# The scan's decays in PSUM, its C rows in SBUF, and one bank for the first stage's matmuls: a two-layer Mamba, attention and expert kernel

## The chip, the cores and the metric

The kernel runs on one core of a Trainium2 chip. Its time is device microseconds from launch to end. Five engines take part: PE (TensorE, matmuls), DVE (VectorE), ACT (ScalarE), POOL (GpSimd) and SP (SyncE, which issues most DMAs). Each works through its own queue in order, and they wait for one another through semaphores. SBUF is the working memory; PSUM is the small memory of eight banks that matmuls write into, and which DVE and ACT can read and write, too. One bank holds a tile of 128 partitions x 512 float32 values.

## What is computed

Eight batch rows of 512 tokens with 256 channels pass two layers. Layer 0 is a gate-and-average conditioning, a Mamba block, a per-row linear map and a mixture of 8 experts (top 2). Layer 1 is a LoRA-modified feed-forward, attention with 8 heads, an adapter with layer norm, and a mixture of 32 experts (top 4). The change touches the scan of the Mamba block:

```python
delta = jax.nn.softplus(jnp.einsum('blr,dr->bld', dt, W_dt) + b_dt)
A = -jnp.exp(A_raw)

def step(h, inp):
    x_t, dlt, B_t, C_t = inp
    dA = jnp.exp(dlt[:, None, :] * A[None])
    h = dA * h + dlt[:, None, :] * B_t[:, :, None] * x_t[:, None, :]
    y_t = jnp.einsum('bn,bnd->bd', C_t, h) + D * x_t
    return (h, y_t)
...
_, ys = jax.lax.scan(step, h0, xs)
y = ys.transpose(1, 0, 2) * jax.nn.silu(z)
return jnp.einsum('bld,md->blm', y, W_out)
```

There are 512 inner channels (index d) and 16 states (index n), so 8192 recurrences over 512 time steps for each batch row.

## The kernel before

**Threads.** Two generators are woven together. `thread_x` does the conditioning and the Mamba block of one row after another and writes the result to `xa[b]`. `thread_y` takes the rows in groups [0], [1, 2], [3, 4, 5], [6, 7] through the rest of layer 0 and the attention. While `thread_y` works on one group, the main loop advances `thread_x` through the next group in proportion to the costs that both yield. After the last group of `thread_x`, `top4`'s routes take its place beside `thread_y`; the expert tiles and the gathers of the last mixture end the program. Within `thread_x`, `scan(b)` of one row is woven with `head(b + 1)` of the next: two steps of the head at each yield of the scan, and what is left of the head before item 58 of the scan.

The text order is not yet the order on an engine. The program's framework puts the instructions into the engines' queues when the program is built, by their dependencies, their place in the text and the buffers that are free; in the trace 174 of the 512 scans stand directly behind another scan on DVE, though the text alternates scan and product.

**The scan.** A row's work has 64 items (j, g, k): j is a quarter of the channels (128), g a quarter of the states (4), k a quarter of the 128 channels (32). An item is a tile of 128 partitions (4 states x 32 channels) x 512 time steps.

- `begin(i)` (L619) issues, two items ahead, the decay `dA = exp(delta * A)` on ACT (L623) into one of four SBUF buffers, and `h = (delta * x) * B` on POOL (L625) into one of eight `h` buffers. Both read `packed`, a tile that a DMA has spread over the four state groups (L595, `get_pack`). The B row spread over the partitions, `B4`, comes from `get_B4` (L598): a matmul of the selection matrix `states(g)` with the row's B and C values (`bc3`, bfloat16) into a `gx` bank, then a copy on ACT (L603) into SBUF. It is made once for each g of a row and kept over the four j.
- `run(i)` (L645) issues the recurrence on DVE (L651, `tensor_tensor_scan`, in place over `h`) and the product with the C row (L652). The C row is spread by a matmul for every j and g into the one PSUM bank `c4` (L649, L650), so 16 times for each row, and read there by four products.
- `add(i)` (L654) sums over the states after each four items: four matmuls with `fold` into a quarter each of the bank `yp` (L660). After the last g, DVE adds D x (L664) and POOL multiplies with silu(z) (L665).

**The head.** `head_a` and `head_b` make the next row's inputs of the scan. Each matmul result goes through `gx()` (L373), a PSUM tile of a ring of two banks, and is read by ACT or DVE: 19 such tiles in `head_a` (eight of them for the averages, read by DVE at L475), 13 in `head_b`. `scan` takes two more at its end for `W_out`, and `get_B4` four for each row.

**PSUM.** The pool `psx` of `thread_x` has four banks: `gx` twice, `c4` and `yp`. The pool of `thread_y` has the other four: `g` twice and `acc` twice. The routes of `top4` use `psx` after `thread_x`: `gx` as a ring of two (L938), `yp` and `c4` for the shared expert's sums (L985).

Of the kernel before, what the change touches and what calls it, by code (L numbers as in the profile page):

```python
# [10 lines left out]
F32 = mybir.dt.float32  # L11
I32 = mybir.dt.int32
AF = mybir.ActivationFunctionType
ALU = mybir.AluOpType
# [3 lines left out]
P = 128  # L18
# [33 lines left out]
def adaln_attn_ffn_kernel(ctx: ExitStack, tc: tile.TileContext, d: dict, out: bass.AP):  # L52
# [314 lines left out]
    def thread_x(wp, wk, ps):  # L367
# [3 lines left out]
            return t  # L371

        def gx():  # L373
            return ps.tile([P, T], F32, tag="gx", name="gx", bufs=2)

        rows = {}

# [206 lines left out]
        def states(g):  # L584
            return quads[:, g].rearrange("k n c -> k (n c)")

        packs = [dram.tile([4, P, 2, T], F32, name=f"pack{i}", tag=f"pack{i}") for i in range(2)]
        xzs = [dram.tile([P, 4, 2, T], F32, name=f"xzs{i}", tag=f"xzs{i}") for i in range(2)]
        got, B4s = {}, {}

        def get_pack(b, j, k):

# [2 lines left out]
            nc.sync.dma_start(t, src[None].to_broadcast([4, 32, 2, T]))  # L595
            got[b, j, k] = t

        def get_B4(b, g):  # L598

            pt = gx()  # L600
            mm(pt, [(states(g), rows[b])])
            t = wk.tile([P, T], F32, tag="B4", name="B4", bufs=4)
            nc.scalar.copy(t, pt)  # L603
            B4s[b, g] = t


        fold = wp.tile([P, 32], F32, tag="fold", name="fold")
# [3 lines left out]

        def scan(b):

            bc3 = rows[b]
            items = [(j, g, k) for j in range(4) for g in range(4) for k in range(4)]
            yps, Cs, hs, dAs, xz = {}, {}, {}, {}, {}
            y8 = wk.tile([P, 4, T], F32, tag="y8", name="y8")

            def begin(i):  # L619
                j, g, k = items[i]  # L620
                t = got[b, j, k]
                dA = wk.tile([P, T], F32, tag="dA", name="dA", bufs=4)
                nc.scalar.activation(dA, t[:, 0, :], AF.Exp, scale=A[:, 4 * j + k, g : g + 1])  # L623
                h = wk.tile([P, T], F32, tag="h", name="h", bufs=8)
                nc.gpsimd.tensor_tensor(h, t[:, 1, :], B4s[b, g], ALU.mult)  # L625
                hs[i], dAs[i] = h, dA
                if (g, k) == (1, 0):
                    xz[j] = wk.tile([P, 2, T], F32, tag="xz", name="xz")
                    nc.sync.dma_start(xz[j], xzs[b % 2][:, j])
                if j == 0 and g < 3 and k == 1:  # L630
                    get_B4(b, g + 1)

                if j < 3 and (g, k) == (2, 3):
                    get_pack(b, j + 1, 0)
                if j < 3 and g == 3 and k < 3:
                    get_pack(b, j + 1, k + 1)
                if j == 3 and b + 1 < NB and g == 3:
                    if k == 0:
                        get_pack(b + 1, 0, 0)
                    if k < 3:  # L640
                        get_pack(b + 1, 0, k + 1)
                    if k == 3:
                        get_B4(b + 1, 0)

            def run(i):  # L645
                j, g, k = items[i]
                h = hs[i]
                if k == 0:
                    Cs[0] = ps.tile([P, T], F32, tag="c4", name="c4")  # L649
                    mm(Cs[0], [(states(4 + g), bc3)])  # L650
                nc.vector.tensor_tensor_scan(h, dAs.pop(i), h, 0.0, ALU.mult, ALU.add)  # L651
                nc.vector.tensor_tensor(h, h, Cs[0], ALU.mult)  # L652

            def add(i):  # L654

                j, g, k = items[i]
                if g == 0:
                    yps[j] = ps.tile([P, T], F32, tag="yp", name="yp")
                for k in range(4):
                    nc.tensor.matmul(  # L660
                        yps[j][32 * k : 32 * k + 32, :], fold, hs.pop(i + k), start=(g == 0), stop=(g == 3))
                if g == 3:
                    y = wk.tile([P, T], F32, tag="tr", name="y", bufs=2)
                    nc.vector.scalar_tensor_tensor(y, xz[j][:, 0, :], col("D", j), yps.pop(j), ALU.mult, ALU.add)  # L664
                    nc.gpsimd.tensor_tensor(y8[:, j, :], xz.pop(j)[:, 1, :], y, ALU.mult)  # L665

            begin(0)
            begin(1)
            for i in range(64):
                if i == 58:  # L670
                    yield from after[0]
                if i < 62:
                    begin(i + 2)
                run(i)
                if i % 4 == 0 and i > 0:
                    add(i - 4)
                if i % 2:
                    yield 5
            add(60)
            x = wk.tile([P, KC, T], F32, tag="gm", name="xr")  # L680
            nc.sync.dma_start(x, d["x"][b])
            for e in range(KC):
                pt = gx()
                mm(pt, [(W_out[:, j, ts(e, P)], y8[:, j, :]) for j in range(4)])
                nc.vector.tensor_tensor(x[:, e, :], x[:, e, :], pt, ALU.add)
            nc.sync.dma_start(xa[b], x)
            yield 3
# [6 lines left out]
        yield from head_b(0)  # L694
        for k in range(4):
            get_pack(0, 0, k)
        get_B4(0, 0)

        def head(b):
            yield from head_a(b)  # L700
# [228 lines left out]
    def top4(wp, wk, ps):  # L929
# [5 lines left out]
            nc.sync.dma_start(sh[n], d[n])  # L935

        def ps_tile():
            return ps.tile([P, T], F32, tag="gx", name="g4", bufs=2)  # L938

        xs = []  # L940
        counts = Counts(wp, E4)
        def route(b):
            x = wp.tile([P, KC, T], F32, tag=f"x{b}", name=f"x{b}")
            nc.sync.dma_start(x, xb[b])
            xs.append(x)
            s = dynamic(b, 1)
            dw = wk.tile([P, KC, P], F32, tag="dw", name="dw")
            nc.sync.dma_start(dw, d["dw"][bass.ds(s, 1)].rearrange("s p k o -> p (s k) o"))
            uw = wk.tile([P, C], F32, tag="uw", name="uw")
            nc.sync.dma_start(uw, d["uw"][bass.ds(s, 1)].rearrange("s p o -> p (s o)"))  # L950
            av = wk.tile([P, 7], F32, tag="av", name="av")
            nc.sync.dma_start(av, d["av"][bass.ds(s, 1)].rearrange("s p o -> p (s o)"))
            pt = ps_tile()
            mm(pt, [(dw[:, k, :], x[:, k, :]) for k in range(KC)])
            z = wk.tile([P, T], F32, tag="z", name="z")
            nc.scalar.activation(z, pt, AF.Relu, bias=av[:, 0:1])
            yield 1
            y = wk.tile([P, KC, T], F32, tag="y", name="y4")
            for e in range(KC):
                pt = ps_tile()  # L960
                mm(pt, [(uw[:, ts(e, P)], z)])
                nc.vector.scalar_tensor_tensor(y[:, e, :], pt, av[:, 1 + e : 2 + e], x[:, e, :], ALU.add, ALU.add)
            yield 1
            c, rstd = yield from layernorm(wk, ps_tile, y, bufs=2)
            yield 1
            for k in range(KC):
                nc.vector.scalar_tensor_tensor(c[:, k, :], c[:, k, :], av[:, 3 + k : 4 + k], rstd, ALU.mult, ALU.mult)
                nc.vector.tensor_scalar(c[:, k, :], c[:, k, :], av[:, 5 + k : 6 + k], None, ALU.add)

            yield 1  # L970
            pt = ps_tile()
            lp = pt[:, 0 : 4 * E4].rearrange("p (a e) -> p a e", a=4)
            for a in range(4):
                mm(lp[:, a, :], [(c[:, k, ts(a, P)], gW[:, k, :]) for k in range(KC)])
            pr = softmax(wk, lp, E4, 1.0)
            top = wk.tile([P, 4, 8], F32, tag="top", name="top")
            ti = wk.tile([P, 4, 8], U32, tag="ti", name="ti")
            for a in range(4):
                nc.vector.max(top[:, a, :], pr[:, a, :])
                nc.vector.max_index(ti[:, a, :], top[:, a, :], pr[:, a, :])  # L980
            nc.vector.tensor_copy(wts4[:, b], top[:, :, 0:K4])
            yield from dispatch(b, c, ti, dest4, counts, wk, ps_tile, ps_tile, E4, K4, CAP4, tab4, "tab4")

            yield 1
            yp = [ps.tile([P, T], F32, tag=t, name="y4p") for t in ("yp", "c4")]  # L985
            for f in range(KC):
                pa = ps_tile()
                mm(pa, [(sh["Ws1"][:, k, ts(f, P)], c[:, k, :]) for k in range(KC)])
                pb = ps_tile()
                mm(pb, [(sh["Ws3"][:, k, ts(f, P)], c[:, k, :]) for k in range(KC)])  # L990
                a = wk.tile([P, T], F32, tag="a", name="a4", bufs=2)
                nc.scalar.activation(a, pa, AF.Silu)
                nc.vector.tensor_tensor(a, a, pb, ALU.mult)
                for k in range(KC):
                    nc.tensor.matmul(yp[k], sh["Ws2"][:, f, ts(k, P)], a, start=(f == 0), stop=(f == KC - 1))
                yield 1
            for k in range(KC):
                nc.vector.tensor_tensor(x[:, k, :], x[:, k, :], yp[k], ALU.add)
# [202 lines left out]
```

## Time and profile before

| what | value |
|---|---|
| median of 3 runs | 4290.34 us (4277.67 to 4293.29) |
| the profiled execution | 4282.53 us, of which its span is 4280.8 us |
| busy PE, DVE, ACT, POOL | 3470.1, 2667.8, 1683.1, 1570.6 us |
| mean granted TensorE clock | 0.886 |
| scans (L651) | 512, first at 145.5 us, last at 2924.8 us |
| decays (L623) | 512, 720 ns each, and 86 table loads of 1283 ns |
| B copies (L603) | 32, 578 ns each |
| fold matmuls (L660) | 1024 |

The span is the time from the first to the last instruction that the profiler saw. An engine's busy time is the union of its instructions' times. In a cost group, the two numbers behind the first bar are the busy time of all and the mean time of one in ns; behind the second bar is the time that the engine stood idle before them, and which instruction's end released it. "PE" is matmuls, "PEld" the weight loads ahead of them.

The rows follow each other so: head 0 alone to 145.5 us; scan 0 with head 1 to 392.8; from there scans 1 to 7 with later heads and `thread_y`, the scans starting at 392.7, 716.2, 1047.0, 1396.4, 1746.9, 2087.6 and 2611.7 us; the routes and the last group of `thread_y`; and from about 3850 us the last expert tiles and gathers.

### The profile page before, as it was taken

The page shows a single profiled execution, that of the slowest core. Times are in us where ns is not written, and L with a number is a line of the kernel's source. Part 1 is how long each engine was busy: PE and PEld are TensorE (multiplying, and loading weights), DVE is VectorE, ACT ScalarE, POOL GpSimd, SP SyncE. Part 2 cuts the span into 40 slices and gives each one's busy share as a digit, 9 for nine tenths or more (in the row PEclk, how much of TensorE's full clock was granted, in tenths as well). Part 3 has the DMA queues.
Part 4 walks back from the last instruction along what each step waited for, and adds up shares of the span by engine and source line. Part 5 has one row for each costly group of instructions (what it writes and reads, how often), then busy time and mean ns, then how long its engine had stood idle before and what let it go on. Part 6 is the DMA issues. An engine that isn't in the chain of part 4 may idle for free. (4 is left out here: it accounts for less than half of the span.)

```text
span 4280.8 us, 36836 instructions
## 1 busy us (share of the span) xinstructions
PE 3470.1 (81%) x10964; PEld 1699.2 (40%) x10964; DVE 2667.8 (62%) x4276; ACT 1683.1 (39%) x2753; POOL 1570.6 (37%) x1222
## 2 busy tenths in 40 slices
PE   4557686888687888888858898889988999977994
PEld 2111352332254233333327443333456444436773
DVE  5698957987866686796791547565432354443336
ACT  2535463454355345346433443332223243222222
POOL 0456535435536334433552323231043211124552
PEclk7668798898798898999879998999999999989996
DMA  3325445234446423333346312213043212117776
GB/s 104 120 91 194 180 153 172 99 116 165 161 162 210 140 100 117 128 117 106 138 169 226 125 62 70 74 35 104 15 160 137 90 44 70 36 44 243 249 239 221
DMA packets 159372, 554.78 MB, mean 130 GB/s; under 512 B 27730, under 2 KB 34289, under 8 KB 146756
## 3 DMA queue, kind: packets, MB, share of 16 engines
q1 hardware_dynamic: 135076, 501.35, 34.8%
q0 software_dynamic: 24096, 51.08, 3.2%
q8 instruction: 87, 1.43, 0.1%
q14 instruction: 113, 0.93, 0.1%
HBM read 453.00 MB, written 234.82 MB: 161 GB/s over the span
## 5 line engine op out<-in xcount | busy, mean ns | idle before, releaser
L625 POOL TENSOR_TENSOR h<-packed,B 128x512 f32<-128x512 f32 x512 | 790.7, 1566 | 1045.0 <-PE yp L660 669.6
L651 DVE TENSOR_TENSOR_SCAN h<-dA,h 128x512 f32<-128x512 f32 x512 | 799.0, 1585 | 142.8 <-POOL h L625 77.3
L623 ACT ACTIVATE dA<-packed,Aexp 128x512 f32<-128x512 f32 x512 | 360.5, 720 | 676.5 <-DVE h L651 468.1
L160 POOL DMA_INDIRECT tok<-ys,to_i x310 | 312.5, 1008 | 494.4 <-DVE ys L808 228.1
L660 PE MATMUL yp<-h,fold 128*32 128x512 f32 x1024 | 355.2, 710 | 166.2 <-DVE h L652 151.8
L922 PE MATMUL acc<-aT,V 128*128 128x512 f32 x1024 | 454.4, 598 | 8.2 <-ACT aT L906 4.9
L160 POOL DMA_INDIRECT tab<-row,si x192 | 199.6, 1040 | 463.0 <-DVE si L250 170.0
L652 DVE TENSOR_TENSOR h<-h,c 128x512 f32<-128x512 f32 x512 | 329.8, 672 | 24.2 <-PE c L78 23.3
L922 PEld LDWEIGHTS acc<-aT,V 128*128 128x128 f32 x1024 | 193.2, 191 | 248.9 <-issue 236.0
L78 PE MATMUL acc<-wv,c 128*128 128x512 f32 x512 | 276.2, 655 | 2.7 <-DVE aT L906 2.0
L78 PE MATMUL g<-qk 64*128 64x512 f32 x512 | 228.2, 673 | 59.1 <-ACT qk L871 32.0
L892 DVE TENSOR_REDUCE nm<-g 128x1 f32<-128x512 f32 x256 | 170.2, 681 | 122.4 <-PE g L78 121.3
L895 ACT ACTIVATE ex<-g,nm 128x512 f32<-128x512 f32 x256 | 175.0, 686 | 163.8 <-DVE nm L892 162.6
L78 PE MATMUL g<-xT,fw 128*128 128x256 f32 x960 | 234.4, 396 | 0.4 <-ACT h L801 0.4
L78 PE MATMUL acc<-fw,h 128*128 128x256 f32 x960 | 221.6, 383 | 4.1 <-DVE ys L808 2.4
L78 PEld LDWEIGHTS g<-xT,fw 128*128 128x128 f32 x960 | 187.8, 200 | 38.7 <-issue 8.0
L905 PEld LDWEIGHTS acc<-ident,ex 128*128 128x128 f32 x1024 | 126.5, 149 | 188.1 <-issue 69.7
L78 PEld LDWEIGHTS acc<-fw,h 128*128 128x128 f32 x960 | 182.6, 192 | 42.4 <-issue 12.2
L905 PE MATMUL acc<-ident,ex 128*128 128x128 f32 x1024 | 163.8, 291 | 41.2 <-ACT V L879 26.8
L660 PEld LDWEIGHTS yp<-h,fold 128*32 128x32 f32 x1024 | 45.2, 116 | 374.4 <-DVE h L652 217.6
L479 DVE TENSOR_TENSOR_SCAN tr<-alpha,gm 128x512 f32<-128x512 f32 x128 | 182.4, 1442 | 7.4 <-POOL y L665 7.1
L78 PE MATMUL g<-xT,mw 128*128 128x256 f32 x760 | 183.9, 386 | 0.0
(280 smaller groups left out, 5437.8 us busy)
## 6 DMA issues: line engine op xcount, KB each, us to landing
fw<-in_fW SPq DMA_DIRECT2D x60, 1154.0 KB
tab<-zeros SPq DMA_DIRECT2D x32, 2112.0 KB
packed<-pack SPq DMA_DIRECT2D x128, 512.0 KB
mw<-in_mW SPq DMA_DIRECT2D x95, 384.0 KB
tab<-zeros SPq DMA_DIRECT2D x16, 2080.0 KB
xt<-tab SPq DMA_DIRECT2D x95, 264.0 KB
xz<-xzs SPq DMA_DIRECT2D x32, 512.0 KB
pack<-dd SPq DMA_DIRECT2D x32, 512.0 KB
```

Of the source, the lines that this page charges most:

```text
L78: nc.tensor.matmul(o, lhsT, rhs, start=(i == 0), stop=(i == len(pairs) - 1))
L160: i = nc.gpsimd.indirect_dma_start(out=table_, out_offset=bass.IndirectOffsetOnAxis(ap=idx, axis=0), in_=src, in_offset=None, bounds_check ...
L479: nc.vector.tensor_tensor_scan(tr, alpha[:, 1 + i : 2 + i].to_broadcast([P, T]), gm[:, k, :], 0.0, ALU.mult, ALU.add)
L623: nc.scalar.activation(dA, t[:, 0, :], AF.Exp, scale=A[:, 4 * j + k, g : g + 1])
L625: nc.gpsimd.tensor_tensor(h, t[:, 1, :], B4s[b, g], ALU.mult)
L651: nc.vector.tensor_tensor_scan(h, dAs.pop(i), h, 0.0, ALU.mult, ALU.add)
L652: nc.vector.tensor_tensor(h, h, Cs[0], ALU.mult)
L660: nc.tensor.matmul(yps[j][32 * k : 32 * k + 32, :], fold, hs.pop(i + k), start=(g == 0), stop=(g == 3))
L892: nc.vector.tensor_reduce(nm, sp, AX.X, ALU.max, negate=True)
L895: nc.scalar.activation(ex, sp, AF.Exp, bias=nm, accum_out=den)
L905: nc.tensor.transpose(tp[:, m, :], ex[:, ts(m, P)], ident)
L922: nc.tensor.matmul(ys[k], V[:, m, C * u + P * k : C * u + P * (k + 1)], aTs[u][:, m, :], start=(u == 0 and m == 0), stop=(u == 1 and m == 3))
```

## The change

Three things are done at once; the eight banks of PSUM are in use before and after:

- `dA` moves from four SBUF buffers to two PSUM banks. ACT writes it there, and the scan on DVE reads it there.
- The C rows are made beside the B rows, once for each g of a batch row, by the renamed `get_rows`: a matmul into `gx` and a copy on ACT into SBUF, where they stay over the four j. The product of L652 reads them there. The bank `c4` and its matmuls in `run` are gone.
- `gx` has one bank instead of two. In `top4` the names follow: the ring of two is now `dA`, and the second sum is `gx`.

```diff
         def gx():
-            return ps.tile([P, T], F32, tag="gx", name="gx", bufs=2)
+            return ps.tile([P, T], F32, tag="gx", name="gx", bufs=1)
...
-        def get_B4(b, g):
-
-            pt = gx()
-            mm(pt, [(states(g), rows[b])])
-            t = wk.tile([P, T], F32, tag="B4", name="B4", bufs=4)
-            nc.scalar.copy(t, pt)
-            B4s[b, g] = t
+        def get_rows(b, g):
+
+            for t, u in (("B4", g), ("C4", 4 + g)):
+                pt = gx()
+                mm(pt, [(states(u), rows[b])])
+                q = wk.tile([P, T], F32, tag=t, name=t, bufs=4)
+                nc.scalar.copy(q, pt)
+                four[t, b, g] = q
...
-                dA = wk.tile([P, T], F32, tag="dA", name="dA", bufs=4)
+                dA = ps.tile([P, T], F32, tag="dA", name="dA", bufs=2)
                 nc.scalar.activation(dA, t[:, 0, :], AF.Exp, scale=A[:, 4 * j + k, g : g + 1])
                 h = wk.tile([P, T], F32, tag="h", name="h", bufs=8)
-                nc.gpsimd.tensor_tensor(h, t[:, 1, :], B4s[b, g], ALU.mult)
+                nc.gpsimd.tensor_tensor(h, t[:, 1, :], four["B4", b, g], ALU.mult)
...
                 if j == 0 and g < 3 and k == 1:
-                    get_B4(b, g + 1)
+                    get_rows(b, g + 1)
...
                     if k == 3:
-                        get_B4(b + 1, 0)
+                        get_rows(b + 1, 0)
...
             def run(i):
                 j, g, k = items[i]
                 h = hs[i]
-                if k == 0:
-                    Cs[0] = ps.tile([P, T], F32, tag="c4", name="c4")
-                    mm(Cs[0], [(states(4 + g), bc3)])
                 nc.vector.tensor_tensor_scan(h, dAs.pop(i), h, 0.0, ALU.mult, ALU.add)
-                nc.vector.tensor_tensor(h, h, Cs[0], ALU.mult)
+                nc.vector.tensor_tensor(h, h, four["C4", b, g], ALU.mult)
...
         def ps_tile():
-            return ps.tile([P, T], F32, tag="gx", name="g4", bufs=2)
+            return ps.tile([P, T], F32, tag="dA", name="g4", bufs=2)
...
-            yp = [ps.tile([P, T], F32, tag=t, name="y4p") for t in ("yp", "c4")]
+            yp = [ps.tile([P, T], F32, tag=t, name="y4p") for t in ("yp", "gx")]
```

More of the change, by code (lines that the diff above doesn't have):

```diff
@@ L588, in thread_x @@
         xzs = [dram.tile([P, 4, 2, T], F32, name=f"xzs{i}", tag=f"xzs{i}") for i in range(2)]
-        got, B4s = {}, {}
+        got, four = {}, {}
         def get_pack(b, j, k):
@@ L612, in scan @@
         def scan(b):
-            bc3 = rows[b]
             items = [(j, g, k) for j in range(4) for g in range(4) for k in range(4)]
-            yps, Cs, hs, dAs, xz = {}, {}, {}, {}, {}
+            yps, hs, dAs, xz = {}, {}, {}, {}
             y8 = wk.tile([P, 4, T], F32, tag="y8", name="y8")
@@ L696, in thread_x @@
             get_pack(0, 0, k)
-        get_B4(0, 0)
+        get_rows(0, 0)
         def head(b):
```

## The prediction

> **What bounds the kernel now.** I read the engine totals, then the busy table by stage, then the cost groups, the minimum/median/maximum of the tiles concerned, the waits, and last the DVE and POOL rows in order of time. The stages were cut where the first scan of each batch row starts (145.5, 392.8, ... us) and where the last scan ends (2926). The chain that ended last is of no use here: it names only the tail of the program (the tok scatters and the last gathers), and the change lies before 2926 us.
>
> ```profile
> core 0: us, PE busy (x) PEld busy (x) DVE busy (x) ACT busy (x) POOL busy (x), PEclk, DMA share, GB/s
> 145.50:392.80 247.30, 149.41 (x258) 34.35 (x258) 225.20 (x200) 113.25 (x146) 144.23 (x88) 0.71 0.34 125
> 392.80:716.20 323.40, 234.04 (x731) 119.07 (x729) 242.70 (x308) 154.40 (x217) 166.69 (x119) 0.80 0.52 178
> ...
> 1047.00:1396.50 349.50, 254.56 (x894) 141.62 (x890) 244.83 (x357) 175.95 (x245) 175.37 (x133) 0.84 0.53 182
> ...
> 2087.60:2611.70 524.10, 433.50 (x1488) 237.54 (x1485) 301.49 (x515) 211.42 (x348) 189.76 (x149) 0.90 0.40 138
> ```
>
> Row 0's scan is bound by DVE (225 of 247 us, 91%). Rows 1 to 5, where the second thread fills in, have DVE at 70 to 81% and PE at 72 to 87%: neither is full, and each waits for the other. In row 6's stage PE leads with 83%.
>
> ```profile
> L651 DVE TENSOR_TENSOR_SCAN h<-dA,h x512: 1181/1214/9431, 145.5 to 2924.8; 128x512 f32<-128x512 f32 x171
> L625 POOL TENSOR_TENSOR h<-packed,B x512: 1250/1299/3663, 144.2 to 2919.9; 128x512 f32<-128x512 f32 x171
> L652 DVE TENSOR_TENSOR h<-h,c x512: 648/675/689, 146.8 to 2929.1; 128x512 f32<-128x512 f32 x171
> ...
> L651 DVE TENSOR_TENSOR_SCAN h<-dA,h 128x512 f32<-128x512 f32 x512 | 799.0, 1585 | 142.8 <-POOL h L625 77.3 <-ACT dA L623 65.4
> L625 POOL TENSOR_TENSOR h<-packed,B 128x512 f32<-128x512 f32 x512 | 790.7, 1566 | 1045.0 <-PE yp L660 669.6
> L78 PE MATMUL c<-bc,quads 96*128 96x512 bf16 x128 | 55.6, 435 | 51.9 <-DVE h L652 49.7 <-ACT bc L337 1.9
> ```
>
> The scan's median is 1214 ns but its mean is 1585; POOL's multiply has 1299 against 1566. The product that follows the scan never exceeds 689 ns. Something stretches the first two and leaves the third alone. In order of time:
>
> ```profile
> 1300.14 2.48 DVE L652 TENSOR_TENSOR h<-h,c 128x512 f32<-128x512 f32 x4 [3.42 <-PE c L78]
> 1302.54 7.62 DVE L651 TENSOR_TENSOR_SCAN h<-dA,h 128x512 f32<-128x512 f32 x4
> ...
> 1301.17 6.80 POOL L625 TENSOR_TENSOR h<-packed,B 128x512 f32<-128x512 f32 x4 [1.92 <-PE yp L660]
> ```
>
> Four scans take 7.62 us (1.9 each) while POOL multiplies, and POOL takes 1.7 per multiply. Taken one by one over the trace, the 226 scans with no POOL work beside them last 1206 ns on average, the 286 others 1885. The products have 672 in both cases, and so, at 738 to 742, has the y of L664, which like the product has one tensor in PSUM. The excess, 512 x (1585 - 1206) = 194 us of DVE time, comes from two SBUF tensors being read beside POOL.
>
> ```profile
> ACT dA L623 <- DVE h L651: 468.1, 229, 11.9
> ...
> PE yp L660 <- DVE h L652: 151.8, 48, 8.4
> ...
> POOL h L625 <- ACT B L603: 66.5, 11, 15.4
> ...
> PE c L78 <- DVE h L652: 49.7, 22, 8.1
> ...
> PE gx L78 <- DVE gm L475: 48.0, 15, 10.0
> ```
>
> PE stands 151.8 us for products that DVE delivers late, and 49.7 us because the single c bank is not yet read out. ACT waits 468 us for dA buffers even with four of them, but few wait for ACT in turn: 65.4 us by the scan.
>
> [...] scalar_tensor_tensor takes 740 ns with PSUM (L664) and 734 or 742 without (L484, L531, undisturbed). [...] no ACT instruction writes PSUM in this trace. [...] the trace has 86 loads at L623 of 1283 ns each.
>
> **The change part by part.**
>
> *Scan with dA in PSUM.* One SBUF input is left. All 512 fall to the undisturbed 1206: -194 us of DVE. [...]
>
> *Product with C4 in SBUF.* Two SBUF inputs now, 672 ns undisturbed (L564, two SBUF tensors, has 684). It inherits the contention. Upper bound: at 217 of the 512 starts a POOL multiply is in flight, and what is left of it adds up to 189 us. The same count for the scans gives 191 us against the 194 seen, so it is a fair measure. But many of these multiplies were late only because a scan had held them: ended 1262 ns after their start, they leave 130 us. And POOL waits for folded products before it starts (669.6 us), so its bursts fall on the next scans, which are now free. I halve the 130: +65 us. Bounds 0 and 189. Net DVE: -129 us.
>
> What a saved DVE microsecond is worth, by stage: 0.9 in row 0, 0.6 in rows 1 to 5, 0.35 in rows 6 and 7; these are my choices after the busy shares. The scan excess by row is 35, 26, 22, 31, 17, 18, 25, 22 us, of which two thirds (129/194) stay saved: 24 x 0.9 + 75 x 0.6 + 31 x 0.35 = 21 + 45 + 11 = 77 us.
>
> *C rows.* 128 matmuls become 32: 96 x 0.435 = 42 us of PE, and the 49.7 us wait on the c bank goes. Of 91 us I count 0.35, since PE also waits for DVE: 32 us. ACT gets 32 copies like L603, 32 x 0.578 = 18.5 us, on an engine 45% busy from 145 to 2926 us: nothing. They are issued with the B rows, through the same bank one after the other; no DMA moves, and no SP queue is passed.
>
> *POOL.* Multiplies no longer held by scans shorten from 1566 toward 1300. The scan waits 77.3 us for them; I take off 20 (0 to 50).
>
> *gx with one bank.* Each row has 19 gx tiles in head_a, 13 in head_b, 2 for W_out, and 8 B and C tiles: 336 in all. Now a matmul waits until its forerunner is read out. Head 0 lies bare on the path: the first W_in half has matmuls 1.2 and ACT reads 1.46 in series against 2.2 of DVE, +0.5 three times; the second half +0.7 three times; W_dt +0.66 three times; four pairs in head_a +0.4 each: 7 us. The other 300 lie beside scans; PE, standing at such a matmul, holds the second thread's matmuls behind it. The wait exists today (gm, 48.0 us). I take 0.1 us each, 30 us, bounds 0 and 100.
>
> *dA with two banks.* The exp of item i+2 can start only after scan i. Until scan i+1 ends DVE has 1.2 us, with a product 1.9, and the exp takes 0.72. That covers it unless ACT is switching tables: out and back is 2 x 1.283 us plus two activations. Behind the held exp stand the second thread's Gelu and copies, for which PE waits. I take 20 us, bounds 0 and 120 (86 loads x 1.4 us uncovered). A faster exp into PSUM is counted at nothing.
>
> After 2926 us the same count of banks serves the routes under other names: nothing.
>
> Sum: -77 - 32 - 20 + 7 + 30 + 20 = -72 us. The profiled execution took 4282.5 us (span 4280.8), so it would be 4210.5; the median of the runs is 7.8 higher, hence 4218. What then is late next: PE's fold waiting for the product, and the second thread's PE work.
>
> **The rivals.** *B, the contention vanishes* (POOL's bursts fall wholly on scans): 194 x 0.8 + 91 x 0.5 - 20 = about 180 us gained, 4110. For it: POOL starts after folds. Against it: only 182 of 512 products follow another product and 84 follow a scan, so head and second-thread work is mixed in and the phases drift. *C, it only changes place*: products wait the full 189, 5 us of DVE stay (worth 3), PE's 32 stay, the costs of 57 remain: +22, 4312. For it: the count of 217 starts. Against: the scans no longer hold POOL. *D, slower, the two short rings*: ACT, in order, stands at an exp for its dA bank; the gx readers behind it come late, PE stands at the next gx matmul, and no fold or second-thread matmul passes. Price: 120 us for the uncovered table switches plus 336 x 0.3 = 100 for gx, with head 0's 7, against 129 gained: +98, 4388. It decides once the two exceed about 150 us, where I take 50. For it: 229 of 512 exps wait already with four buffers, and single banks already cost PE 49.7 us at c. Against it: few wait for ACT today.
>
> **How the numbers follow.** The main case has 0.44 (4150 to 4268 by itself), B 0.21, C 0.13, D 0.22. The range of 4105 to 4345 leaves out the lower part of B and the upper half of D. A difference of 0.5% (21 us) is about what a measurement of this kernel can tell from none. Faster: main and B, 0.65. Same: most of C, 0.12. Slower: D and the rest of C, 0.23.
>
> **What would show it.** Right: scans near 1210 ns mean and maximum; products above 672 in the mean, by about 130 ns; POOL multiplies near 1300; 32 C matmuls; row 0's stage some 20 us shorter. Wrong: products at 1000 ns or more (C); scans waiting well over 65 us for ACT, L623 table loads far above 86, or PE's waits at gx grown to several times 48 us (D)[...].

## The result, and the profile after

The changed kernel takes 4319.37 us (median of 4 runs, 4316.32 to 4321.78), against 4284.01 us for the kernel before in runs that now include one more. The ratio is 1.0082, with an interval of 1.0065 to 1.0099: 35 us slower, where 72 us less had been forecast. The profiled execution took 4316.32 us, of which its span is 4314.5.

The stages of the changed kernel first, cut where its first scan starts and its last scan ends. The columns are those of the stage table shown before.

```profile
core 0: us, PE busy (x) PEld busy (x) DVE busy (x) ACT busy (x) POOL busy (x), PEclk, DMA share, GB/s
0.00:178.70 178.70, 76.88 (x140) 27.90 (x141) 65.76 (x103) 50.96 (x66) 22.35 (x30) 0.73 0.32 91
178.70:2957.90 2779.20, 2189.10 (x6387) 950.87 (x6386) 1939.46 (x2656) 1334.53 (x2042) 1072.62 (x816) 0.87 0.38 131
2957.90:4314.50 1356.60, 1186.27 (x4343) 696.90 (x4341) 571.47 (x1521) 373.58 (x724) 372.23 (x377) 0.94 0.39 129
```

The same cut of the kernel before:

```profile
0.00:145.50 145.50, 70.92 (x145) 27.75 (x145) 69.99 (x104) 54.61 (x70) 22.04 (x30) 0.76 0.37 110
145.50:2926.00 2780.50, 2207.21 (x6497) 971.77 (x6497) 2026.87 (x2654) 1255.79 (x1961) 1176.69 (x815) 0.87 0.38 131
2926.00:4280.80 1354.80, 1191.99 (x4323) 699.63 (x4322) 570.94 (x1520) 372.70 (x723) 371.90 (x377) 0.93 0.39 128
```

All of the loss lies in head 0, before the first scan: 178.7 us instead of 145.5. The middle is as long as before, to 1.3 us, although DVE is busy 87 us less in it and PE 18 us less. So two questions stand: why head 0 costs 33 us, and what took the middle's 87 us of DVE back. The scan itself did what was expected, in the cost groups (busy us, mean ns, then idle time before):

```profile
L625 POOL TENSOR_TENSOR h<-packed,B 128x512 f32<-128x512 f32 x512 | 713.1, 1415 | 1052.2 <-PE yp L657 586.9
L648 DVE TENSOR_TENSOR_SCAN h<-dA,h 128x512 f32<-128x512 f32 x512 | 612.0, 1210 | 216.7 <-POOL h L625 142.9
L649 DVE TENSOR_TENSOR h<-h,C 128x512 f32<-128x512 f32 x512 | 440.0, 878 | 8.9 <-ACT C L604 6.6
```

The scan fell from 1585 to 1210 ns, POOL's multiply from 1566 to 1415, and the product rose from 672 to 878: the 210 products with POOL work beside them last 1168 ns on average, the other 302 last 677. What rose beside them are the waits around the `gx` bank; of each line the total, the number and the longest are given in us:

```profile
POOL h L625 <- ACT B L604: 140.4, 22, 15.6
...
DVE h L648 <- POOL h L625: 142.9, 59, 7.8
...
PE gx L78 <- DVE gm L475: 96.4, 30, 7.5
...
PE gx L78 <- DVE dd L560: 34.1, 14, 7.3
...
PE gx L78 <- ACT sz L540: 33.0, 12, 7.8
...
PE gx L78 <- ACT B L604: 21.4, 14, 7.0
...
PE gx L78 <- ACT C L604: 15.3, 12, 3.9
```

Before, the waits for gm, dd, sz and B were 48.0, 21.9, 11.8 and 6.0 us. All of PE's idle time before `gx` matmuls after the first scan went from 135 to 244 us: PE now stands for the reader of the only bank. POOL's wait for the B rows went from 66.5 to 140.4 us, and the scan's wait for POOL from 77.3 to 142.9.

### The profile page after: what moved, and what is told of

It is laid out like the page before. It is cut to its first block, busy times and chain, and to the rows that moved or that the text cites. A ratio compares the mean times of both kernels' runs of the same rounds, so it can differ in the third digit from the quotient of the medians.

```text
span 4314.5 us, 36602 instructions
## 1 busy us (share of the span) xinstructions
PE 3452.2 (80%) x10868; PEld 1675.7 (39%) x10868; DVE 2576.7 (60%) x4279; ACT 1759.1 (41%) x2832; POOL 1467.2 (34%) x1222
## 5 line engine op out<-in xcount | busy, mean ns | idle before, releaser
L625 POOL TENSOR_TENSOR h<-packed,B 128x512 f32<-128x512 f32 x512 | 713.1, 1415 | 1052.2 <-PE yp L657 586.9
L648 DVE TENSOR_TENSOR_SCAN h<-dA,h 128x512 f32<-128x512 f32 x512 | 612.0, 1210 | 216.7 <-POOL h L625 142.9
L623 ACT ACTIVATE dA<-packed,Aexp 128x512 f32<-128x512 f32 x512 | 349.6, 690 | 662.7 <-DVE h L648 529.7
L649 DVE TENSOR_TENSOR h<-h,C 128x512 f32<-128x512 f32 x512 | 440.0, 878 | 8.9 <-ACT C L604 6.6
L78 PE MATMUL g<-qk 64*128 64x512 f32 x512 | 239.8, 684 | 40.9 <-ACT ex L892 30.2
L78 PE MATMUL gx<-cen,W_in 128*128 128x512 f32 x256 | 147.5, 702 | 57.2 <-DVE cen L513 25.0
```

The source lines that it names most:

```text
L78: nc.tensor.matmul(o, lhsT, rhs, start=(i == 0), stop=(i == len(pairs) - 1))
L625: nc.gpsimd.tensor_tensor(h, t[:, 1, :], four["B4", b, g], ALU.mult)
L649: nc.vector.tensor_tensor(h, h, four["C4", b, g], ALU.mult)
```

## The experiments

Three theories were tried. *gx*: the single bank for the head's matmuls takes back what the scan gains. *ring*: two decay buffers are too few. *place*: the contention has only moved to the product. The runs were made on three chips, where the kernel before has medians of 4319, 4310 and 4279 us; each ratio is against the kernel before on the same chip. An unchanged run on the second shows where it differs from the chip of the first profile:

> The kernel before, unchanged, for a profile on the chip of these runs. Expected: the stages to the last scan as in the first profile within 10 us, and any difference of the whole in the part after the last scan, which was 25 to 40 us longer in every run on this chip.

Head 0 took 147.3 us, the scans 2779 us, and the part after them 1384 us in place of 1355. So it is that part, and the runs on the chip of 4319 us have 1381 to 1395 us there. The stages up to the last scan, and ratios within a chip, can be compared.

**One bank alone.** In the kernel before:

```diff
-            return ps.tile([P, T], F32, tag="gx", name="gx", bufs=2)
+            return ps.tile([P, T], F32, tag="gx", name="gx", bufs=1)
```

> The kernel before with one gx bank in place of two, and nothing else (the routes at the end keep a ring of two banks under two names). Theory gx (the single bank costs head 0 its 33 us and, in the middle, about what the scans gain): first scan near 178 us, PE's idle time before gx matmuls after that up from 135 to some 240 us, and the whole 60 to 130 us slower than before. Theory ring (two dA buffers eat the gain) and theory place (the products' new contention eats it): only head 0's 33 us, so 25 to 45 us slower.

It took 4479.92 us, ratio 1.0371 (1.0354 to 1.0388), 161 us slower. The theory gx had expected 60 to 130 us and the others no more than 45; the cost is above even the former. Its stages, and then POOL's wait for the B rows and PE's largest wait for a bank:

```profile
0.00:175.60 175.60, 75.50 (x141) 27.26 (x141) 65.83 (x103) 50.96 (x66) 22.37 (x30) 0.76 0.32 92
175.60:3090.10 2914.50, 2265.11 (x6502) 980.57 (x6502) 2027.31 (x2661) 1331.05 (x2012) 1165.75 (x815) 0.86 0.36 125
3090.10:4472.30 1382.20, 1199.00 (x4323) 701.02 (x4322) 571.94 (x1519) 373.65 (x724) 372.89 (x377) 0.93 0.38 126
```

```profile
POOL h L625 <- ACT B L603: 142.3, 21, 15.4
PE gx L78 <- DVE gm L475: 97.7, 25, 13.3
```

Head 0 has its 30 us here, too, and the middle is 134 us longer with the same 2027 us of DVE work. This one edit costs four and a half times the whole loss. By the ratios, the rest of the change is therefore worth 1.0082 / 1.0371 = 0.972, a gain of some 125 us beside one `gx` bank. What it would gain beside two was not measured: that takes a ninth bank beside the eight of the two pools.

**Two decay buffers alone.** In the kernel before, `bufs=4` of `dA` became `bufs=2`.

> The kernel before with two dA buffers in SBUF in place of four, and nothing else. Theory ring: 40 to 100 us slower, with the scans' idle time behind ACT well over the 65 us of before and more table loads at L623 than 86. Theory gx and theory place: within 15 us of before.

4331.98 us, ratio 1.0026 (1.0014 to 1.0039): 11 us. The signs of the theory ring came in part (the scan's wait for ACT rose from 65 to 120 us, the table loads at L623 from 86 to 93), but not its 40 us or more, so it falls as the main cause.

**The scan writes into its bank.** In the changed kernel:

```diff
-                nc.vector.tensor_tensor_scan(h, dAs.pop(i), h, 0.0, ALU.mult, ALU.add)
-                nc.vector.tensor_tensor(h, h, four["C4", b, g], ALU.mult)
+                dA = dAs.pop(i)
+                nc.vector.tensor_tensor_scan(dA, dA, h, 0.0, ALU.mult, ALU.add)
+                nc.vector.tensor_tensor(h, dA, four["C4", b, g], ALU.mult)
```

> The changed kernel with the scan writing into its dA bank, so that the product reads one tensor in PSUM and one in SBUF: neither the scan nor the product has two SBUF inputs. All else as in the changed kernel, but a dA bank is held until the product is done. Expected of every theory: scans near 1210 ns, products near 680 ns in place of 878, DVE busy about 100 us less. Theory place: 60 us or more faster than the changed kernel, so some 4255 us. Theory gx: 0 to 25 us faster than the changed kernel. Theory ring: slower than the changed kernel, since the ring is held longer.

4303.22 us, ratio 0.9962 (0.9949 to 0.9975), so 0.9962 / 1.0082 = 0.988 of the changed kernel, about 52 us less. The product is back at 678 ns, and DVE's busy time in the middle at 1854 us, 85 less than in the changed kernel. The gain lies between what place and gx had allowed: the product's contention is a real cost, but a third of the single bank's.

**Head 0 through other banks.** In the changed kernel, head 0's matmuls use the second thread's ring `g` (`lone[0]` is true until head 0 is done):

```diff
         def gx():
+            if lone[0]:
+                return psy.tile([P, T], F32, tag="g", name="gx", bufs=2)
             return ps.tile([P, T], F32, tag="gx", name="gx", bufs=1)
```

> The changed kernel, but the matmuls of head 0 alone go to the two banks g of the second thread, which has not begun then. Every theory: the first scan is back at 145 to 148 us. If head 0 is a cost of its own, the whole is 30 to 35 us faster than the changed kernel, near 4286, equal to before within 10 us. If the delay of head 0 is hidden later, less than 10 us are gained.

4335.27 us, ratio 1.0031 (1.0017 to 1.0045), 0.995 of the changed kernel: 22 us, of the 30 to 35 expected. Head 0 was back at 149 us, but the scans took 2789 us, 10 more than in the changed kernel. So most of head 0's loss is a cost of its own, to be added to what the scans lose.

**One ring of three.** In the changed kernel, the `gx` bank and the two `dA` banks became one ring (in the routes, the second sum takes a bank of that ring):

```diff
-            return ps.tile([P, T], F32, tag="gx", name="gx", bufs=1)
+            return ps.tile([P, T], F32, tag="dA", name="gx", bufs=3)
...
-                dA = ps.tile([P, T], F32, tag="dA", name="dA", bufs=2)
+                dA = ps.tile([P, T], F32, tag="dA", name="dA", bufs=3)
```

> The changed kernel with its three banks gx, dA, dA put into one ring that both the first stage's matmuls and the decays draw from. The number of banks is the same; head 0 can have all three. Theory gx (one bank for the matmuls is what costs): first scan back at about 146 us, middle 40 to 100 us shorter, so 1.5 to 3% faster than the changed kernel and 1 to 2% faster than before. Theory place (the products' contention is what costs): head 0's 30 us and no more, so equal to before within 0.3%. If decays and matmuls take each other's banks: no faster than the changed kernel.

4255.71 us, ratio 0.9879 (0.9843 to 0.9916), 0.980 of the changed kernel. Its first two stages, its scan and its product:

```profile
0.00:145.70 145.70, 67.68 (x141) 27.90 (x142) 66.58 (x104) 51.75 (x68) 21.92 (x30) 0.77 0.38 110
145.70:2877.20 2731.50, 2188.51 (x6386) 961.44 (x6385) 1946.64 (x2652) 1277.83 (x2006) 1073.85 (x815) 0.86 0.39 133
...
L648 DVE TENSOR_TENSOR_SCAN h<-dA,h 128x512 f32<-128x512 f32 x512 | 612.0, 1209 | 202.2 <-ACT dA L623 139.7
...
L649 DVE TENSOR_TENSOR h<-h,C 128x512 f32<-128x512 f32 x512 | 460.5, 912 | 4.0
```

With the same eight banks, the change turns from 0.8% slower into 1.2% faster: first scan at 146 us, the middle 48 us shorter than the changed kernel's. The products still take 912 ns. So the contention of the product does not decide the sign; the place for the matmuls does. The ring can give the decays a third bank, too, but the scan's wait for them rose from 73.5 to 139.7 us, so they are not what gained; the scan's wait for POOL fell from 142.9 to 58.8.

**Ring and bank together.**

> The ring of three and the scan that writes into its dA bank, together. If the two costs are separate, the gains add: another 1 to 1.5% below the ring alone, so 2 to 3.5% faster than before. If the bank that is held until the product is done starves the matmuls of the ring, it is no faster than the ring alone.

4179.27 us, ratio 0.9697 (0.9667 to 0.9728): 131 us faster than before, the fastest kernel of this study, and 1.8% below the ring alone. The gains add, within the intervals (0.980 x 0.988 = 0.968 of the changed kernel was to be expected; 0.9697 / 1.0082 = 0.962 came). Its stages, and then its scan and product with minimum, median and maximum:

```profile
0.00:144.20 144.20, 66.39 (x141) 27.56 (x141) 66.59 (x104) 51.66 (x68) 21.91 (x30) 0.76 0.39 111
144.20:2803.30 2659.10, 2166.34 (x6408) 959.70 (x6409) 1834.45 (x2654) 1282.76 (x2015) 1013.59 (x815) 0.87 0.40 137
```

```profile
L649 DVE TENSOR_TENSOR_SCAN dA<-dA,h x512: 1193/1219/1232, 144.2 to 2802.1; 128x512 f32<-128x512 f32 x171
L650 DVE TENSOR_TENSOR h<-dA,C x512: 652/678/693, 145.4 to 2803.8; 128x512 f32<-128x512 f32 x171
```

Neither row has a long tail any more: no scan above 1232 ns, no product above 693, with POOL at work beside 286 of the scans and 258 of the products. The middle is 121 us shorter than before.

**Other banks for two heads, with the scan in its bank.** Heads 0 and 1 and scan 0's rows use `g`, one `gx` bank from there on.

> The scan that writes into its dA bank, and the matmuls of heads 0 and 1 and of scan 0's rows go to the two banks g of the second thread, which has not begun then; one gx bank from there on. Theory gx: first scan back at 146 us, scan 0's stage 10 to 20 us shorter, so 30 to 45 us faster than the scan in the bank alone, 1.0 to 1.4% faster than before.

4272.18 us, ratio 0.9912 (0.9884 to 0.9941): 0.995 of the scan in the bank alone, some 22 us where 30 to 45 were expected. The first scan was back at 146 us, but scan 0's stage did not shorten (257.9 us, against 254.2 with the scan in the bank alone). This kernel is still 93 us slower than the ring and the bank together, where the matmuls of every head can take up to three banks.

**Is it the bank, or the function tables?** With one bank the count of ACT's table loads rose from 284 to 339, perhaps because the head's activations come one at a time between exps. In the trace of before they take 1283 ns each; the one at 144.89 us, for example, stands between an Exp (L623) and a Ln (L569), and 193 of the 284 are at the lines of the head and of the scan's exps. Two runs compute the head with Tanh in place of Gelu, Sigmoid, Silu and Ln, and so other values, with two banks and with one.

> The kernel before with every Gelu, Sigmoid, Silu and Ln of the head replaced by Tanh (so the head computes other values), so that the head shares a function table with the scan's exps. It is the base for the next run. Expected: table loads 284 down to some 120 to 170, and a time 20 to 100 us below before.

> The same replacement by Tanh in the head, and one gx bank in place of two. If the matmuls' single bank costs by itself (PE stands until the bank is read), it is 90 us or more slower than the run with Tanh and two banks, of the 160 us that one bank cost with the true functions. If most of the 160 us were the 55 added table loads, it is 20 to 70 us slower than that run, with nearly equal table loads.

The base has 109 loads against 284, fewer than expected, and takes 4259.91 us, ratio 0.9956 (0.9939 to 0.9972). With one bank there are 125 loads and 4354.5 us, ratio 1.0163 (1.0127 to 1.0199): 95 us more than its base, with 16 more loads (21 us of ACT time). Head 0 is again 31 us longer in the profiles, the middle 86. So most of the cost doesn't need the table loads: some 95 us came almost without them. Whether the 55 added loads make up the other 66 of the 161 us is not shown. Two chips lie between the numbers, and 175 loads fewer, 225 us of ACT time at 1283 ns, brought the base itself only 20 us, which speaks against it.

**Sharing alone.** In the kernel before, `gx` twice and `c4` in one ring of three.

> The kernel before with its three banks gx, gx and c4 put into one ring, and nothing else. If sharing banks gains by itself, it is 0.8% or more faster than before, and the ring of three in the changed kernel owes its gain to that. If not, it is within 0.4% of before.

4311.77 us, ratio 1.0076 (1.005 to 1.0101). It is slower, which no theory had expected; its middle took 2806 us. So a shared ring doesn't gain by itself, which speaks for the ring of three gaining in the changed kernel because it undoes the single bank. The two rings are not quite alike: here the matmuls share with `c4`, which is held for four products, and there with the decays.

## Why the prediction was wrong

- *The scan* was right: -194 us expected, 512 x (1585 - 1210) = 192 measured; 1210 ns with the decay in PSUM is within 4 of the 1206 undisturbed in SBUF.
- *The product* was undersized. +65 us were taken; 512 x (878 - 672) = 105 came, within the bounds of 0 and 189. In the new trace 149 products start while POOL multiplies, and what is left of these multiplies, the prediction's own measure, adds up to 114 us. It was the halving from 130 to 65 that failed: POOL's bursts moved to the scans less than thought. Net DVE is -87 us where -129 were forecast.
- *What a DVE microsecond is worth*: taken as 0.35 to 0.9, 0.6 for rows 1 to 5. The scan in its bank removed 85 us of DVE time and 52 us of the whole: 0.6, though POOL's multiplies also shortened there, from 1415 to 1346 ns. The 0.9 for row 0 finds no support: its stage was to be 20 us shorter and went from 247.3 to 259.6 us.
- *The C rows*: the matmuls for B and C rows fell from 70.4 to 28.7 us, the 42 us counted, and the wait at `c` is gone. PE's idle time before `gx` matmuls grew by 110 us beside it. No run prices the C rows alone.
- *The decays' two banks*: 20 us taken, 11 measured for two buffers in SBUF. The table switches at L623 rose to 93, not far above 86. This half of rival D didn't come.
- *POOL*: the scan's wait for it was to shrink by 20 us, and grew by 66. The multiplies did shorten, but they wait for the B rows: 140.4 us, and 142.3 with one bank alone, where no C row passes through it, so the added C rows are not needed for that. With ring and bank together it is 164.7 us, and yet the scan waits only 57.6 us for POOL: the wait for the B rows alone does not tell the cost.
- *gx* is the step that failed: "7 us" for head 0 and "0.1 us each, 30 us" for the rest. Alone, the edit costs 161 us, of which, by the profiles, 30 are head 0 and 134 the middle (0.49 us for each of the 272 tiles that this kernel has after head 0, 38 for each row; above the 0.3 of rival D). With 161 in place of 37 the sum of the prediction would have been +52 us, against 35 measured: the sign was lost in this one term. The other terms add up to 77 + 32 + 20 - 20 = 109 us of gain, against some 125 from the ratios, but that is partly luck, since DVE saved less and POOL's wait grew.
- *The rivals*: D named the queue behind the one bank and underpriced it. Of its signs, PE's wait for gm only doubled, to 96.4 us, where several times 48 had been named. C's 4312 us lies near the result, but not for its reason: the products grew by 105 us, not by 189.

Head 0's error could have been seen. I took 1.2 us for the matmuls of a W_in tile: two of 0.592. But the trace of before has 256 such matmul records for 64 tiles, four to a tile. PE's timeline over the eight W_in tiles, before:

```profile
94.19 11.86 PE L78 MATMUL gx<-cen,W_in 128*128 128x512 f32 x20 [5.32 <-DVE cen L513]
106.98 5.70 PE L78 MATMUL gx<-cen,W_in 128*128 128x512 f32 x12 [0.94 <-ACT xc L529]
```

And after:

```profile
110.56 3.78 PE L78 MATMUL gx<-cen,W_in 128*128 128x512 f32 x4 [5.32 <-DVE cen L513]
115.78 3.68 PE L78 MATMUL gx<-cen,W_in 128*128 128x512 f32 x4 [1.45 <-ACT xc L529]
120.91 1.98 PE L78 MATMUL gx<-cen,W_in 128*128 128x512 f32 x4 [1.45 <-ACT xc L529]
124.39 1.98 PE L78 MATMUL gx<-cen,W_in 128*128 128x512 f32 x4 [1.50 <-ACT xc L529]
127.87 1.98 PE L78 MATMUL gx<-cen,W_in 128*128 128x512 f32 x4 [1.50 <-ACT xc L529]
131.97 2.92 PE L78 MATMUL gx<-cen,W_in 128*128 128x512 f32 x4 [2.12 <-ACT sz L540]
135.66 3.78 PE L78 MATMUL gx<-cen,W_in 128*128 128x512 f32 x4 [0.78 <-ACT sz L540]
140.27 1.98 PE L78 MATMUL gx<-cen,W_in 128*128 128x512 f32 x4 [0.83 <-ACT sz L540]
```

A tile takes 1.98 us at best and up to 3.78, and each after the first now waits 0.8 to 2.1 us for ACT's last read. The eight tiles stretch from 18.5 to 31.7 us: 13 of the 33 us, in a place where I had counted 3.6. With 1.98 for a tile my sum for these eight would have been 5.8 us in place of 3.6 (1.98 + 1.46 in series against DVE's 2.2, and ACT's 0.68, three times each). Another 4.5 us are matmul time: PE is busy for 22.1 us with the eight tiles, and was for 17.5 before. The last 3 us are waits beyond that sum. The other 20 us of head 0 were not taken apart, but most of its loss is waits of this kind: PE's idle time before all `gx` matmuls of head 0 rose from 69 to 101 us.

In the middle the error was the wrong measure. I priced a tile by what PE loses at it, and looked for cover in the second thread's work. But the bank joins the queues of PE, ACT and DVE. In the changed kernel, a matmul for the averages ended at 1586.8 us, DVE read it (gm) only at 1593.7, after scans and products, and PE stood 5.5 us before the next matmul into the bank. What follows on PE waits, too: later PE stood 4.5 us before a W_in matmul for ACT's read (sz), to 1709.8 us, and the second thread's matmuls of aT and V, both complete since 1697.1, went on only behind it, at 1713.3. PE's own waits before `gx` matmuls after the first scan rose from 135 to 210 us in the run with one bank, by 76; the middle by 134. How the rest splits among the engines stays open. Part of it can be that the order in the queues is made anew when a ring changes, which no run here separates; the shared ring in the kernel before, 0.8% slower against every theory, shows that such an edit can move the time by that much.

## What to carry to other kernels

- When a buffer moves into a scarce memory, price first the ring that gives up a bank: with one bank, a producer and its readers run in series, as the W_in tiles above (0.8 to 2.1 us of wait at each after the first), and what is queued behind them waits, too. Here that cost 161 us, more than the 125 that the move was worth.
- Before halving a ring, try to let two users share the banks: the same three banks as one ring were 2% faster than as one and two. It is no rule, since in the kernel before, one ring of three was 0.8% slower than two and one.
- The contention that came with two SBUF operands (beside POOL, 1885 ns against 1206 for the scan before, 1168 against 677 for the product after) was removed for a whole chain by leaving the intermediate in PSUM: the scan in place in its bank freed the product, too (678 ns), and gained 1.2%.

## What was not expected of the hardware

- The exp is faster into PSUM, but the gain is small: 690 ns in the changed kernel, against 720 into SBUF before.
- A PSUM operand cost the scan next to nothing: the scan that reads and writes PSUM takes 1218 ns (ring and bank together), the one that reads PSUM and writes SBUF 1210, undisturbed in SBUF 1206.
- Table loads on ACT were cheap in the kernel before, where ACT is busy for 39% of the span: 175 fewer, of 1283 ns each, brought 0.4%.
